# A decoder layer on one core: early tiles and late gates in the front, split score exponentials and shared row work at the end

## The chip, the cores and the metric

The kernel runs on one core of a Trainium2 chip. TensorE (PE) does the matmuls and transposes, VectorE (DVE) and ScalarE (ACT) the element-wise work and the evacuation of PSUM, GpSimd (POOL) part of the element-wise work in SBUF, and SyncE (SP) issues most of the DMAs. The metric is the device time of one execution in microseconds (us), as the median of several runs.

## The reference

One decoder layer in fp32, for 16 sequences `x` of 512 × 256, with a context of 64 × 128 for each. `_layernorm` is a layernorm without weights.

```python
# 1. long-convolution block with a gated MLP (FF = 672)
z = rmsnorm(u, pre_norm_w) @ in_proj_w.T              # 256 -> 768 channels
z_pre = depthwise_causal_conv3(z, short_w) + short_b
x2, x1, v = split(z_pre, 3)
h = sum(residues[:, :, None] * exp(log_poles * t), axis=1)   # 16 poles a channel
xv = x1 * v
y = (causal_conv(xv, h) + xv * D_skip) * x2           # x2 is the gate
y = y @ out_proj_w.T + u
zm = rmsnorm(y, post_norm_w)
y = y + gelu(zm @ l1_w.T) * (zm @ l2_w.T) @ l3_w.T
x = _layernorm(x + y)
# 2. causal self attention plus cross attention (16 heads of 16)
y = softmax(causal(q k^T) / 4) v + softmax(qc kc^T / 4) vc
x = _layernorm(x + y @ Wp + bp)
# 3. low-rank FFN: 256 -> 64 -> 1024 -> 64 -> 256
x = _layernorm(x + gelu(x @ U1 @ V1 + b1) @ U2 @ V2 + b2)
```

## The kernel before

**Two plans.** The order of the work is not written by hand. Each step is an operation with the engines that may run it, an estimated cost, a priority (a lower number goes first), and the buffers that it reads and writes. `Plan.schedule` simulates the engines with these costs, and each engine's instructions are emitted in the order found; each engine then runs its queue in order, with semaphores between engines. A buffer comes from a class with a fixed number of tiles, and an operation starts only when a tile of its class is free. So a change of priority, of engine or of the number of tiles moves other work too.

**The front plan** does all that goes before sequence 0 can run. `prepare` (L440) loads x, normalises it and transposes it to `xT`. `project` (L473) makes one of six slices of 128 channels: two matmuls of 512 (L479, two records each, so four records for one projection), an ACT evacuation (L486), and two DVE steps of the short convolution (L494). `x1v` (L502) takes two projections, multiplies them on POOL (L506), transposes the product on PE (L512) and copies it into `xv`, kept on chip. `gate_of` (L523) takes two projections of x2 and stores them to DRAM (`gates`). Poles and residues give the table `h` (L607 to L637: 32 exponentials on ACT, L613, and 32 multiply-adds on DVE, L623), which is stored to DRAM as `hpad`.

The long convolution (L648 to L774) runs in eight blocks, four for each half kh of the channels. A block loads four Toeplitz tiles ("toes", 512 KB each) from `hpad` (L661), clears their upper part on POOL (L671), and runs the near states (L686, then L696, L706 and L714), the exponentials of the far part (L722), the toe matmuls (L737) and the far matmuls (L749); the result is copied to a row and stored to DRAM (`yconv`, L768). Half kh = 0 runs among the projections. Half kh = 1 needs the `xv` of all sequences.

The class `"x"` has ten tiles of 4 KB a partition (`fx` in the profile). It holds the loaded x, the `xT`, and the toes. The last nine sequences (LATE) have only their first x1·v made early, and the last five (KEPT) keep their `xT` until the second one. The gates of sequences 14 and 15 (LAST) are made after the convolution. In the last part of kh = 1 the toes also use the first half of `xv`, which is finished then (class `"x0"`).

**The main plan** pipelines the sequences: `first_block` (loads of x, gate and the two halves of `yt`, gating at L1105, output projection L1118, MLP L1143 to L1195), `attention` and `ffn`, each in a later window, so that three sequences are under way. In attention, `scores` is one tile of four PSUM banks (128 × 2048). A round is: PE writes the scores (L1491; L1552 in the cross attention), ACT takes the exponential of the whole tile into one of three `ex` tiles (L1503, L1563), POOL clears the part above the diagonal (L1514), and PE multiplies by the values (L1526, L1578). The next round's scores need the same tile. A sequence has twelve rounds (ten of L1491, two of L1552). `to_tokens` (L1056) projects the result back, and `layernorm_ops` (L1019) ends each block: statistics on DVE, the inverse root on POOL (L308, L309), the scaling of four rows of tokens on ACT (L1041). `ffn` (L1689) has transposes (L348), L1704, four pairs of blocks (two L1716 into two `mm` banks, two gelus at L1724 on ACT, two L1732 into `av`), and L1745. The last sequence has no later one beside it.

Of the kernel before, what the change touches and what calls it, by code (L numbers as in the profile page):

```python
# [10 lines left out]
AF = mybir.ActivationFunctionType  # L11
# [186 lines left out]
def decoder_layer(  # L198
# [77 lines left out]
    def tiles(home, name, n, shape):  # L276
        return [home.tile(shape, F32, name=f"{name}{k}") for k in range(n)]
# [88 lines left out]
    R8 = 8  # L366
    NR = D // HPG
    with ExitStack() as front:
        fp_ = front.enter_context(tc.tile_pool(name="front", bufs=1))
# [4 lines left out]
            "mm": tiles(fps, "fmm", 8, [P, T]),  # L374
            "x": tiles(fp_, "fx", 10, [P, R8 * P]),
            "far": tiles(fp_, "far", 1, [P, R8, P]),
# [59 lines left out]

        def as_xT():
            return View("x", lambda t: t.rearrange("p (k n) -> p k n", k=KD))

        def prepare(b, pr):  # L440

            x_ = View("x", lambda t: t.rearrange("p (c d) -> p c d", c=NT))
            for c in range(0, NT, 1 if b == 0 else NT):
                cs = slice(c, c + (1 if b == 0 else NT))
                plan.op(
                    "SP", 0.5 if b == 0 else 0.5 * MB,
                    lambda e, cs=cs: nc.sync.dma_start(
                        out=x_.t[:, cs, :], in_=x[b].rearrange("(c p) d -> p c d", p=P)[:, cs, :]
                    ),
                    pr - 1000, w=[(x_, c)] if b == 0 else [x_], lat=2.5, after=at_step(b - 3),  # L450
                )
            if b == 0:
                load_in(prew, pre_w, -900, [(INW, "p")])
                for k in range(KD):
                    load_in(inw[:, k, :], in_wT[bass.ts(k, P), :], -900, [(INW, k)])
                load_in(cw, conv_w, -890, [(CW, 0)])
                load_in(cb, conv_b, -890, [(CW, 1)])
                for k in range(KD):
                    plan.op(
                        "DVE", 0.9,  # L460
                        lambda e, k=k: nc.vector.tensor_scalar(
                            inw[:, k, :], inw[:, k, :], prew[:, k : k + 1], None, ALU.mult
                        ),
                        -900, r=[(INW, "p")], w=[(INW, k)],
                    )

            sq = rms_ops(x_, pr - 120)
            scale_ops(x_, sq, pr - 120, "POOL" if b else "DVE")
            xT = transposed(x_, lambda t: t, pr - 120, as_xT())
            marks.append(plan.ops[-1])  # L470
            return xT
# [85 lines left out]
        for b, xT in late:  # L557
            if b < B - KEPT:
                xT = as_xT()
                plan.op(  # L560
                    "SP", 0.5 * MB,
                    lambda e, b=b, xT=xT: nc.sync.dma_start(
                        out=xT.t.rearrange("p k n -> p (k n)"), in_=normed[b - B + LATE]
                    ),
                    1900 + b, r=[(NORMED, b)], w=[xT], lat=2.5, after=at_step(B - 1 - 2 * (b % 2)),
                )
            late_T.append((b, xT))
            x1v(b, 1, xT, 3000 + b * 100)
            marks.append(plan.ops[-1])
            if b < B - LAST:  # L570
                gate_of(b, xT, 3000 + b * 100)
        last_gates = []
# [34 lines left out]
        for k in range(KD):  # L607
            h = Buf("h")
            for n in range(NS):
# [5 lines left out]
                    ),  # L615
                    160, r=[(LP, 0)], w=[ee],
                )
# [10 lines left out]

                plan.op("DVE", 0.32, add, 160, r=[ee, (LP, 1), (LP, 2)], w=[h])
            plan.op(  # L630
                "SP", 0.4, lambda e, k=k, h=h: nc.sync.dma_start(out=hpad[bass.ts(k, P), :], in_=h.t), 160,
                r=[h], w=[(HPAD, k)], lat=3.0,
            )
        plan.op(
            "SP", 0.4, lambda e: nc.sync.dma_start(out=hpad[D : D + 1, :], in_=zero_row), 160, w=[(HPAD, KD)],
            lat=3.0,
# [9 lines left out]
        plan.op("ACT", 0.4, lambda e: nc.scalar.activation(aT, lpT, AF.Exp, scale=float(P)), 170, r=[(LP, "T0")], w=[(NEAR, "a")])  # L646

        for blk in range(NR // R8):  # L648
            d0 = blk * R8 * HPG
# [105 lines left out]
            for c in range(HPG):  # L755
                o = View("row", lambda t: t.rearrange("p (q u) -> p q u", u=P))
                plan.op(
                    "ACT DVE", (act(T), dve(T)),
                    lambda e, c=c, o=o, ys=ys: copy(
                        e, o.t, ys[c].t.rearrange("p (q u) -> p q u", u=P)[:, :, ::-1]  # L760
                    ),
                    pc + 5, r=[ys[c]], w=[o],
                )
                for par in range(2):

                    def store(e, at=x0 + c * R8 + par * R8 // 2, par=par, kh=kh, o=o):
                        eng = nc.sync if e == "SP" else nc.scalar
                        eng.dma_start(  # L768
                            out=yconv[kh].rearrange("j b d t -> (j b) d t")[:, at : at + R8 // 2, :],
                            in_=o.t[bass.ts(par, 64)],  # L770
                        )


                    plan.op("ACT" if par and blk >= NR // R8 - 3 else "SP", 0.6, store, pc + 10, r=[o], lat=3.0)  # L774

# [204 lines left out]
        "maxes": tiles(kept, "maxes", 2, [P, NT, HPG, SLOT]),  # L980
        "yt": tiles(kept, "yt", 1, [P, KD, T]),
        "gate": tiles(kept, "gate", 1, [P, KD * T]),
        "y1": tiles(kept, "y1", 1, [P, NT, D]),
        "xt": tiles(kept, "xt", 5, [P, NT, D]),
        "xT": tiles(kept, "xT", 3, [P, KD, T]),
# [32 lines left out]

    def layernorm_ops(x, prio, at_once=NT):  # L1019
        for c0 in range(0, NT, at_once):  # L1020
# [16 lines left out]
            for c in range(c0, c0 + at_once):  # L1037

                def norm(e, c=c, small=small):
                    st = small.t  # L1040
                    nc.scalar.activation(  # L1041
                        x.t[:, c, :], x.t[:, c, :], AF.Identity, bias=st[:, c, 9:10], scale=st[:, c, 8:9]
                    )

                plan.op("ACT", act(D, True) + 0.05, norm, prio, r=[small], w=[(x, c)])

# [33 lines left out]
    def first_block(b, after):  # L1080
# [15 lines left out]

        plan.op("SP", 0.5, load_x, p0 - 500, w=[x_], lat=4.0)
        plan.op("SP", 0.5, load_g, p0 - 500, w=[gate], lat=4.0)
        for k in range(KD):
            plan.op("SP", 0.5, lambda e, k=k: load_y(e, k), p0 - 500, w=[(yt, k)], lat=4.0)  # L1100
# [106 lines left out]
    def attention(b, x_):  # L1207
# [241 lines left out]
        def shifted(g):  # L1449
# [8 lines left out]
            for gg in range(g, g + 2):  # L1458
                q = qs[gg]
                qas[gg], cqas[gg] = Buf("q"), Buf("q")  # L1460
                for row, dst in ((self_rows[gg % 2], qas[gg]), (cross_rows[gg % 2], cqas[gg])):
# [6 lines left out]
                    )  # L1468

        def sums(g0):  # L1470

# [10 lines left out]
            for uses in fills:  # L1482
# [3 lines left out]
                def mm(e, uses=uses, sc=sc):  # L1486
                    at = 0
                    for g, j in uses:
# [11 lines left out]
                ))  # L1500
                exps[b + 1].append(plan.op(
                    "ACT", act(HPG * T),
                    lambda e, sc=sc, ex=ex: nc.scalar.activation(  # L1503
                        ex.t.rearrange("p (r n) -> p r n", r=HPG), sc.t, AF.Exp, scale=scale
                    ),
                    pb_ - 5, r=[sc], w=[ex],
                ))
                at = 0
# [34 lines left out]
        def cross_scores(g):  # L1543
# [4 lines left out]
            def cm(e):  # L1548
                for r in range(HPG):
# [10 lines left out]
            ))  # L1560
            exps[b + 1].append(plan.op(
                "ACT", act(HPG * T),
                lambda e: nc.scalar.activation(  # L1563
                    ex.t.rearrange("p (r n) -> p r n", r=HPG), sc.t, AF.Exp, scale=scale
                ),
                pb_ - 5, r=[sc], w=[ex],
            ))

# [116 lines left out]
        to_tokens(yT, wp_s, x_, p3)  # L1685
        layernorm_ops(x_, p3, NT // 2 if b == B - 1 else NT)
        return begun

    def ffn(b, x_):  # L1689
# [18 lines left out]

        acc = Buf("av")
        for fp in range(NH // 2):  # L1710
            hp = [Buf("mm"), Buf("mm")]

            def hm(e, fp=fp, hp=hp):
                for s in range(2):
                    half = bass.ts(s, RANK)
                    nc.tensor.matmul(hp[s].t, v1_s[half, bass.ts(fp, P)], pT.t[half, :], start=True, stop=True)  # L1716

            gelus_pe[window].append(plan.op("PE", tiled(T), hm, p3, r=[pT], w=hp, tiling=ROWS2))
            hT = [Buf("row"), Buf("row")]
            for s in range(2):  # L1720
                f = 2 * fp + s
                gelus[window].append(plan.op(
                    "ACT", act(T, True),
                    lambda e, f=f, src=hp[s], dst=hT[s]: nc.scalar.activation(  # L1724
                        dst.t, src.t, AF.Gelu_apprx_tanh, bias=b1_s[:, f : f + 1]
                    ),
                    p3, r=[hp[s]], w=[hT[s]],
                ))
# [23 lines left out]
        n = NT // halves  # L1752
        layernorm_ops(x_, p4, n)
        for c0 in range(0, NT, n):
# [112 lines left out]
```

## Time and profile before

| | |
|---|---|
| median of the runs | 2112.74 us (2112.03, 2112.74, 2116.0) |
| profiled execution, its own time | 2110.95 us |
| its span in the profile | 2109.2 us |
| mean TensorE clock granted in the profiled execution | 0.987 of full |
| PE busy | 2013.7 us, 95% of the span |
| DVE busy | 1317.1 us, 62% |
| ACT busy | 1020.7 us, 48% |
| POOL busy | 758.2 us, 36% |
| DMA | 182.16 MB, 86 GB/s on average |
| second half of the convolution, first L686 | at 247.78 us |
| first L1118 (sequence 0) | at 292.07 us |
| first and last start of the last sequence's score rounds | 2019.51 and 2060.12 us |

The profile is of one execution. The slices give each engine's busy share in tenths in 40 equal parts of the span, 52.7 us each; PEclk is the granted clock of TensorE. A row of the timeline gives start, duration, engine, source line, operation, output and inputs, shapes and the number of instructions put together (xN); in square brackets stands the idle time ahead of it and what ended it. The chain of waits runs back from the last instruction to what released each step. The busy table by stage has one row for each stretch, and the busy time of each engine in it.

### The profile page before, as it was taken

How to read it: one execution, taken by the hardware profiler on the slowest of the kernel's cores; microseconds unless marked ns; L12 is line 12 of the kernel's file. 1: busy time of each engine (PE TensorE's matmuls, PEld its weight loads, DVE VectorE, ACT ScalarE, POOL GpSimd, SP SyncE). 2: the span in 40 equal slices, each digit the busy share in tenths (PEclk: the TensorE clock that was granted, in tenths of full speed). 3: DMA queues.
4: the chain of work that ended last, by engine and by line, in shares of the span. 5: the costliest groups of instructions: out<-in, count | busy, mean ns of one | idle time of the engine just before them, and what ended most of it. 6: DMA issues, size and time to landing. Idle time of an engine off the chain costs nothing.

```text
span 2109.2 us, 35600 instructions
## 1 busy us (share of the span) xinstructions
PE 2013.7 (95%) x14324; PEld 1034.7 (49%) x14324; DVE 1317.1 (62%) x1899; ACT 1020.7 (48%) x1414; POOL 758.2 (36%) x1020
## 2 busy tenths in 40 slices
PE   8899878999999999999999999999999999999977
PEld 4455545444554545454545454544545454545433
DVE  7976522736584848484847575766656675746463
ACT  7764521565426262717172626262535354466664
POOL 6785522243424241414141424242323232334342
PEclk9999989999999999999999999999999999999999
DMA  5366861030304040313131313222221313030300
GB/s 190 112 199 210 272 191 50 1 122 17 117 11 140 14 132 22 122 32 120 34 109 45 106 48 93 61 86 68 72 81 61 93 49 95 19 105 22 102 11 21
DMA packets 114935, 182.16 MB, mean 86 GB/s; under 512 B 13393, under 2 KB 62034, under 8 KB 114642
## 3 DMA queue, kind: packets, MB, share of 16 engines
q1 hardware_dynamic: 113234, 177.26, 27.0%
q10 hardware_dynamic: 1536, 2.62, 0.4%
q8 instruction: 113, 1.85, 0.4%
q14 instruction: 52, 0.43, 0.1%
HBM read 111.09 MB, written 68.76 MB: 85 GB/s over the span
## 4 chain that ended last, share of the span: by engine, by line
PE 81%; ACT 7%; POOL 4%; DVE 3%; issue 3%; DMA 2%; SPq 0%; ACTq 0%; POOLq 0%; DVEq 0%
PE mm L1143 14%; PE scores L1387 10%; PE mm L1296 9%; PE mm L1195 8%; PE scores L1491 7%; PE av L1526 7%; PE mm L1716 4%; PE mm L1224 3%; PE av L1732 3%; PE mm L1056 3%; PE fmm L479 2%; ACT ex L1503 2%; PE mm L1118 2%; PE mm L348 2%; PE mm L1578 2%
## 5 line engine op out<-in xcount | busy, mean ns | idle before, releaser
L1503 ACT ACTIVATE ex<-scores 128x2048 f32<-128x2048 f32 x160 | 300.2, 1876 | 165.4 <-PE scores L1491 161.3
L1143 PE MATMUL mm<-xT,w_l 128*128 128x512 f32 x640 | 298.1, 607 | 0.0
L1514 POOL TENSOR_SCALAR_AFFINE_SELECT ex<-ex 128x512 f32<-128x512 f32 x256 | 158.6, 638 | 355.2 <-ACT ex L1503 330.8
L1387 PE MATMUL scores<-keys,q 32*128 32x320 f32 (+4 forms) x2560 | 224.2, 455 | 11.8 <-ACT ex L1406 10.4
L1491 PE MATMUL scores<-q,keys 32*128 32x512 f32 (+3 forms) x2048 | 185.0, 464 | 17.3 <-ACT ex L1503 14.2
L1724 ACT ACTIVATE row<-mm,b_s 128x512 f32<-128x512 f32 x128 | 81.0, 685 | 233.0 <-PE mm L1716 232.9
L1143 PEld LDWEIGHTS mm<-xT,w_l 128*128 128x128 f32 x640 | 114.9, 190 | 143.7 <-issue 130.8
L1387 PEld LDWEIGHTS scores<-keys,q 32*128 32x128 f32 x2560 | 113.0, 184 | 147.2 <-issue 48.0
L1660 POOL TENSOR_TENSOR nd<-nd,nd 128x1024 f32<-128x1024 f32 x30 | 70.8, 2361 | 307.4 <-DMA nd<-di 307.4
L479 PE MATMUL fmm<-fx,inw 128*128 128x512 f32 x384 | 176.5, 602 | 4.1 <-DVE xv L299 1.5
L1526 PE MATMUL av<-ex,va 128*32 128x512 f32 (+3 forms) x2048 | 170.8, 442 | 0.0
L1432 DVE TENSOR_TENSOR scores<-scores,mask_qk 128x1024 f32<-128x1024 f32 x144 | 126.2, 876 | 63.8 <-PE scores L1387 60.6
L308 POOL TENSOR_SCALAR small<-small 128x4 f32<-128x4 f32 (+1 forms) x66 | 13.3, 201 | 423.0 <-DVE small L1026 393.7
L494 DVE SCALAR_TENSOR_TENSOR frow<-fmm,cw,frow 128x511 f32<-128x511 f32 x192 | 140.5, 744 | 37.7 <-ACT frow L486 33.5
L1195 PE MATMUL mm<-w_l,gT 128*128 128x256 f32 x640 | 160.8, 386 | 0.0
L1155 ACT ACTIVATE row<-mm 128x512 f32<-128x512 f32 x80 | 47.8, 598 | 223.9 <-PE mm L1143 223.9
L1491 PEld LDWEIGHTS scores<-q,keys 32*128 32x128 f32 x2048 | 90.0, 185 | 117.4 <-ACT ex L1503 42.2
L299 DVE COPY row<-av 128x512 f32<-128x512 f32 x68 | 47.1, 692 | 157.9 <-PE av L1526 136.2
L1195 PEld LDWEIGHTS mm<-w_l,gT 128*128 128x128 f32 x640 | 117.8, 190 | 47.3 <-issue 33.7
L1041 ACT ACTIVATE xt<-xt,small 128x256 f32<-128x256 f32 x192 | 103.1, 595 | 76.6 <-POOL small L1034 76.6
L1302 DVE TENSOR_SCALAR q<-mm,bqc_s 128x512 f32<-128x512 f32 x62 | 46.5, 751 | 140.6 <-PE mm L1296 140.6
L1296 PE MATMUL mm<-xT,wqc_s 128*128 128x512 f32 x256 | 129.3, 617 | 0.0
(194 smaller groups left out, 3475.4 us busy)
## 6 DMA issues: line engine op xcount, KB each, us to landing
dn<-row SPq DMA_DIRECT2D x120, 256.0 KB
keys<-dk SPq DMA_DIRECT2D x64, 256.0 KB
nd<-dn SPq DMA_DIRECT2D x30, 512.0 KB
nd<-di SPq DMA_DIRECT2D x30, 512.0 KB
fx<-hpad SPq DMA_DIRECT2D x28, 512.0 KB
xt<-in_x SPq DMA_DIRECT2D x16, 512.0 KB
gate<-gates SPq DMA_DIRECT2D x16, 512.0 KB
yt<-yconv SPq DMA_DIRECT2D x32, 256.0 KB
```

The lines of the kernel that those rows point to most:

```text
L479: nc.tensor.matmul(ps.t, inw[:, k, bass.ts(m, P)], xT.t[:, k, :], start=(k == 0), stop=(k == KD - 1))
L494: lambda e, lag=lag: nc.vector.scalar_tensor_tensor(t.t[:, lag:], ps.t[:, 0 : T - lag], cw[:, m, 2 - lag : 3 - lag], t.t[:, lag:], ALU.mul ...
L1041: nc.scalar.activation(x.t[:, c, :], x.t[:, c, :], AF.Identity, bias=st[:, c, 9:10], scale=st[:, c, 8:9])
L1143: nc.tensor.matmul(ps.t, w[:, k, bass.ts(f, P)], zT.t[:, k, :], start=(k == 0), stop=(k == KD - 1))
L1195: nc.tensor.matmul(ps.t[:, bass.ts(cc, D)], gT.t[:, f, bass.ts(c, P)] if f < NF else gE.t, w_l3[:, f, :] if f < NF else w_l3e[:, c, :], st ...
L1296: nc.tensor.matmul(ps.t, w[:, k, cols], xT.t[:, k, :], start=(k == 0), stop=(k == KD - 1))
L1387: nc.tensor.matmul(sc.t[:, r, at : at + hi - lo], q.t[hd, bass.ts(i, P)], kk.t[hd, lo:hi], start=True, stop=True,)
L1432: nc.vector.tensor_tensor(diag, diag, mask, ALU.add)
L1491: nc.tensor.matmul(sc.t[:, r, at : at + T - j * P], keys[g].t[hd, TC + j * P : TC + (j + 1) * P], qas[g].t[hd, j * P :], start=True, stop= ...
L1503: lambda e, sc=sc, ex=ex: nc.scalar.activation(ex.t.rearrange("p (r n) -> p r n", r=HPG), sc.t, AF.Exp, scale=scale),
L1514: lambda e, ex=ex, at=at: nc.gpsimd.affine_select(out=ex.t.rearrange("p (r n) -> p r n", r=HPG)[:, :, at : at + P], in_=ex.t.rearrange("p ...
L1526: nc.tensor.matmul(av[g].t[bass.ts(r, SLOT), j * P :], va.t[:, j, h * VS : h * VS + SLOT], ex.t[:, r * T + at : r * T + at + n], start=(j ...
```

## The change

1. Three tiles of 4 KB a partition, `early`, are allocated outside the front's pool. In the front plan they hold the `xT` of sequences 11, 12 and 13. In the main plan they are one of the five `xt` tiles, the `gate` tile and the `yt` tile. The class `"x"` has 7 tiles instead of 10.
2. The exponentials, multiply-adds and stores of the `h` table have priority 500 instead of 160.
3. The gates of sequences 10 to 13 have priority 4700 + 100 b instead of 3000 + 100 b, and the second half of the convolution has 5000 and up.
4. Sequence 0's x, gate and the first half of its `yt` are loaded by DMAs in the front plan, after the last readers of the early tiles and after the stores that they need; the main plan's operations for them are empty, and it loads the second half of `yt`.
5. In the last sequence, each exponential of a scores tile is split: ACT takes the first two banks from PSUM; DVE copies the other two to the `ex` tile, and ACT takes their exponential there.
6. In the last sequence, the scaling of rows after attention and after the FFN may run on ACT or DVE. For sequence 14's FFN it runs on DVE.
7. In the last FFN, the first two pairs of L1716 write to the four banks of the scores tile.

```diff
+    early_ = ctx.enter_context(tc.tile_pool(name="early", bufs=1))
+    early = tiles(early_, "early", 3, [P, NT * D])
...
-            "x": tiles(fp_, "fx", 10, [P, R8 * P]),
+            "x": tiles(fp_, "fx", 7, [P, R8 * P]),
+            **{f"e{n}": [t] for n, t in enumerate(early)},
...
-        def as_xT():
-            return View("x", lambda t: t.rearrange("p (k n) -> p k n", k=KD))
+        def as_xT(b):
+            n = b - (B - KEPT)
+            return View(f"e{n}" if 0 <= n < 3 else "x", lambda t: t.rearrange("p (k n) -> p k n", k=KD))
...
-                gate_of(b, xT, 3000 + b * 100)
+                gate_of(b, xT, (3000 if b < B - LAST - 4 else 4700) + b * 100)
...
-                    160, r=[(LP, 0)], w=[ee],
+                    500, r=[(LP, 0)], w=[ee],
...
+        for n, (dst, src, deps) in enumerate((
+            (early[0].rearrange("p (c d) -> p c d", c=NT), x[0].rearrange("(c p) d -> p c d", p=P), ()),
+            (early[1], gates[0], (stores[0][1], stores[1][1])),
+            (early[2].rearrange("p (k j t) -> p k j t", k=KD, j=NT)[:, 0],
+             yconv[0][:, 0].rearrange("j p t -> p j t"), Y[0]),
+        )):
+            plan.op(
+                "SP", 0.6, lambda e, dst=dst, src=src: nc.sync.dma_start(out=dst, in_=src), 5460, w=[Buf(f"e{n}")],
+                lat=4.0, after=[*deps, *(o for _, o, _ in late_T[LATE - KEPT + n][1].seen)],
+            )
...
-        "yt": tiles(kept, "yt", 1, [P, KD, T]),
-        "gate": tiles(kept, "gate", 1, [P, KD * T]),
+        "yt": [early[2].rearrange("p (k n) -> p k n", k=KD)],
+        "gate": [early[1]],
...
-        "xt": tiles(kept, "xt", 5, [P, NT, D]),
+        "xt": [early[0].rearrange("p (c d) -> p c d", c=NT), *tiles(kept, "xt", 4, [P, NT, D])],
...
+                    if e == "DVE":
+                        nc.vector.tensor_scalar(
+                            x.t[:, c, :], x.t[:, c, :], st[:, c, 8:9], st[:, c, 9:10], ALU.mult, ALU.add
+                        )
+                        return
...
-                plan.op("ACT", act(D, True) + 0.05, norm, prio, r=[small], w=[(x, c)])
+                cost = {"ACT": act(D, True) + 0.05, "DVE": dve(D)}
+                plan.op(on, tuple(cost[e] for e in on.split()), norm, prio, r=[small], w=[(x, c)])
...
-        for k in range(KD):
+        plan.op("SP", 0.5, load_x if b else lambda e: None, p0 - 500, w=[x_], lat=4.0)
+        plan.op("SP", 0.5, load_g if b else lambda e: None, p0 - 500, w=[gate], lat=4.0)
+        if not b:
+            plan.op("SP", 0.5, lambda e: None, p0 - 500, w=[(yt, 0)], lat=4.0)
+        for k in range(0 if b else 1, KD):
...
+        def exponentials(sc, ex, prio):
+            direct, half = (HPG, None) if b < B - 1 else (HPG // 2, HPG // 2)
+            def exp(e, src, rs):
+                dst = ex.t.rearrange("p (r n) -> p r n", r=HPG)
+                nc.scalar.activation(dst[:, rs, :], (sc.t if src else dst)[:, rs, :], AF.Exp, scale=scale)
+            if half:
+                rest = slice(direct, HPG)
+                plan.op(
+                    "DVE", dve(half * T),
+                    lambda e: nc.vector.tensor_copy(
+                        ex.t.rearrange("p (r n) -> p r n", r=HPG)[:, rest, :], sc.t[:, rest, :]
+                    ),
+                    prio, r=[(sc, 1)], w=[(ex, "half")],
+                )
+            exps[b + 1].append(plan.op(
+                "ACT", act(direct * T), lambda e: exp(e, True, slice(0, direct)), prio, r=[(sc, 0)] if half else [sc],
+                w=[(ex, "first")] if half else [ex],
+            ))
+            if half:
+                exps[b + 1].append(plan.op("ACT", act(half * T), lambda e: exp(e, False, rest), prio, w=[ex]))
...
-        layernorm_ops(x_, p3, NT // 2 if b == B - 1 else NT)
+        layernorm_ops(x_, p3, *((NT // 2, "ACT DVE") if b == B - 1 else ()))
...
-        acc = Buf("av")
+        acc, sc4 = Buf("av"), Buf("scores")
...
-            hp = [Buf("mm"), Buf("mm")]
+            in_scores = last and fp < 2
+            hp = [(sc4, 2 * fp + s) for s in range(2)] if in_scores else [Buf("mm"), Buf("mm")]
...
-        layernorm_ops(x_, p4, n)
+        layernorm_ops(x_, p4, n, "ACT DVE" if last else "DVE" if window > B else "ACT")
```

## The prediction, made before the changed kernel ran

> **What bounds it now.** First the page's slices (part 2): which engine is full, and where it is not.
>
> ```profile
> PE   8899878999999999999999999999999999999977
> ...
> PEclk9999989999999999999999999999999999999999
> DMA  5366861030304040313131313222221313030300
> ```
>
> TensorE (PE) is full but for slices 0 to 6 (to 316 us) and the last two, so a gain must come out of the two ends, and only what PE waits for counts there. The middle keeps its order on every engine in the built program. Second, the busy table by stage (columns: us, busy time of PE, PEld, DVE, ACT, POOL, then clock, DMA share, GB/s).
>
> ```profile
> 230.00:236.00 6.00, 6.00 (x18) 2.86 (x17) 5.40 (x8) 5.46 (x13) 1.27 (x1) 1.00 0.89 229
> 236.00:241.00 5.00, 4.56 (x11) 1.71 (x9) 4.62 (x7) 4.41 (x12) 2.85 (x3) 1.00 1.00 386
> 241.00:248.00 7.00, 1.99 (x21) 1.38 (x24) 3.65 (x5) 1.83 (x6) 6.55 (x7) 0.69 0.99 395
> 248.00:255.00 7.00, 6.77 (x201) 6.41 (x195) 1.11 (x2) 0.00 (x0) 5.30 (x10) 0.82 0.66 247
> ...
> 284.00:292.00 8.00, 0.00 (x0) 0.00 (x0) 3.89 (x6) 0.29 (x1) 0.00 (x0) 0.75 0.96 328
> 292.00:300.00 8.00, 6.75 (x16) 5.10 (x16) 2.08 (x3) 1.37 (x6) 0.00 (x0) 0.61 0.99 330
> ```
>
> There are two holes: 241 to 248, ahead of the second convolution half, and 284 to 292, ahead of sequence 0. DMA is nearly full in both. Third, PE's timeline names the waits.
>
> ```profile
> 241.62 0.66 PE L512 MATMUL fmm<-ident,frow 128*128 128x128 f32 x4 [1.07 <-POOL frow L506]
> 245.44 1.12 PE L512 MATMUL fmm<-ident,frow 128*128 128x128 f32 x4 [3.16 <-POOL frow L506]
> 247.78 2.79 PE L686 MATMUL fmm<-xv,near 128*32 128x48 f32 x128 [1.22 <-DVE xv L299]
> ...
> 275.90 7.13 PE L479 MATMUL fmm<-fx,inw 128*128 128x512 f32 x16
> 292.07 6.75 PE L1118 MATMUL mm<-outw,yt 128*128 128x256 f32 x16 [9.04 <-DVE yt L1105]
> ```
>
> Fourth, the chain of waits: the first hole hangs on a Toeplitz load (then POOL's L671 and L506), the second on the read of yconv.
>
> ```profile
> 236.12 6.80 DMA fx<-hpad
> ...
> 283.62 7.53 DMA yt<-yconv
> ```
>
> Last, PE and ACT at the other end, where the last sequence has only part of a partner's work beside it.
>
> ```profile
> 2053.70 1.14 PE L1491 MATMUL scores<-q,keys 32*128 32x512 f32 x8 [1.06 <-ACT ex L1503]
> 2056.90 1.15 PE L1491 MATMUL scores<-q,keys 32*128 32x384 f32 x16
> ```
> ```profile
> 2054.97 1.88 ACT L1503 ACTIVATE ex<-scores 128x2048 f32<-128x2048 f32 x1 [1.32 <-POOL ex L1514]
> 2058.20 1.88 ACT L1503 ACTIVATE ex<-scores 128x2048 f32<-128x2048 f32 x1 [1.35 <-PE scores L1491]
> 2080.02 2.06 ACT L1041 ACTIVATE xt<-xt,small 128x256 f32<-128x256 f32 x4
> 2083.64 1.07 ACT L301 COPY xT<-mm 128x512 f32<-128x512 f32 x2 [1.56 <-PE mm L348]
> ```
>
> With one scores tile, a round is scores 1.15, exp 1.88 and two hand-overs: 3.2 us, as the starts 2053.70 and 2056.90 show. Eight of the twelve rounds stand at this floor; the others wait for other work.
>
> **Front.** The sum is made against the profiled execution: 2110.95 us, span 2109.2 and 1.75 around it; it lies 1.79 below the median of 2112.74. A projection is four L479 records: 7.13 / 4 = 1.78 us.
>
> *Late gates.* In the built order four projections fewer stand ahead of the second half's first L686 (247.78): −7.1 us. Two gates (10, 11) now stand between the last x1·v steps, where PE idled 1.07 + 3.16 + 1.22 = 5.45: up to −12.5 for that start. Two things can take it back: POOL's queue, since L506 stands behind L671, which waits for toes (4.36 us behind the load above), and the DMA queues. In 230 to 248 DMA work is 6×0.89 + 5×1.00 + 7×0.99 = 17.3 of 18 us; four gate stores of 256 KB (1.0 MB at 390 GB/s, 2.7 us) and about three prefetched toes of 512 KB (4.0 us) leave it, so 10.6 us is left for the 5.5 us that PE's work would need there. The other 5.1 has to go ahead of 230, where shares of 0.86 (180 to 205) and 0.79 (205 to 230) leave 8.75 us free. It fits with little to spare, so I take −11, from −12.5 to −4.
>
> *Convolution.* One projection (gate 12) now stands inside the half: +1.8. The cold start goes: the clock was 0.69, then 0.82; 0.18 of 7 us is about −1. With x at 7 tiles instead of 10, five x buffers and x0 feed the half instead of eight and x0. The built order gives a buffer some 8 us of PE work between uses; a load takes 6.30 or 6.80 us in the chain, and L671 1.09, so I take +1.2 for those that come late, 0 to +6. Sum +2.
>
> *After it.* Before, convolution's end to L1118 is 292.07 − 275.90 = 16.2 us, 7.1 of it four projections. Now seven follow, 12.5 us. The first loads of sequence 0 (x, gate, half of yt) have gone out earlier; only yt's second half is left, on SP behind two gate stores (ready some 8 us in), and it should land about 11.7 us in; L1105 (0.70) follows. I take 13.5: −2.7 (−4 to 0). The moved gate load waits on SP for gate 12's last L479, 1.8 us after the convolution's PE end; behind it are yconv stores, thus row buffers, the evacuations and PE. Bound 0 to +2, taken inside the 13.5. With no hole in front, the 16 L1118 cost 4.81, as in the later group at 346.85, not 6.75: −1.9.
>
> *Early part.* PE idles about 9 us from 30 to 175, of which 5.4 lies in 55 to 71, where the h tables (L613, 32 × 395 ns; L623, 30 × 414 ns) fill ACT and DVE. Given later priority they can release that; three tiles fewer can delay the input loads by one landing, about 4. Bounds −5 and +4; I take 0, as both act on the same queue.
>
> Front: −11 + 2 − 2.7 − 1.9 = −13.6.
>
> **End.** *Split exponentials.* No row shows a 1024-wide exp; between 587 ns (512 wide) and 1876 ns (2048) the line gives 1.02 us. The nearest row for the DVE copy of two banks is L1432's 128x1024 on the scores tile, 1.23. In the built order the halves do not run side by side: in each round one waits on the other's semaphore, and PE's next scores on both. The banks are held 1.02 + 1.23 + 0.06 = 2.31 instead of 1.88: +0.43, in eight floor rounds +3.5 (0 if other work sets them, +6 with all twelve and one half exp more at the end).
>
> *Shared rows.* The second norm batch (small ready 2080.48) can start the transposes at 2081.1 instead of 2083.01: −1.9 (0 to −2.3). Of the two xT copies in a row (1.07) one goes to DVE: −0.4. *FFN blocks in score banks:* the last FFN runs 2087.5 to 2097.2. Four pairs of gelus at 1.27 are 5.1 of it, norms of sequence 14 between them 2.3, which leave ACT; but the first gelu waits for four L1716 rather than two, +1.1: −1.2 (−2.3 to +1). Final norms 1.09 to 0.60: −0.5. Sum −4.0.
>
> End: +3.5 − 4.0 = −0.5; ends −4 (split free) and +5 (split dear, little shared).
>
> Two rules of the skill weigh on the end. The row: in 2019.5 to 2024.9 the clock was 0.50 and eight score records took 2.09 us, with single waits of PE of 1.99 and 3.32 us around them; in 2050.5 to 2053.7, PE busy 2.14 of 3.20, it was 1.00 and they took 1.15. The Trainium skill, "TensorE: Matmul & The Clock Gate", section "Part 1: The HAM clock gate", halves the clock only after a whole idle window of about 3.4 us; by it, longer rounds stay warm and cost nothing more. By the row a sparse stretch can be cold: 12 × 0.94 = +11 at worst. The new round, 2.14 of 3.63, is nearer to the warm row (67% busy) than to the cold one (39%), so I add none; one cold round, +0.9, is inside the end's +5. "PSUM — Partial Sum Buffer", section "PSUM bank collisions raise a hardware error", lets two engines work on different banks at once; by that rule, halves side by side would hold the banks 1.23 and bring 8 × −0.65 = −5.2. No run here shows it, and the built waits speak against it.
>
> **The sum.** −13.6 − 0.5 = −14.1: 2110.95 − 14.1 = 2096.9 on the profiled execution's basis, 2112.74 − 14.1 = 2098.6 on the median's, which I give. About 0.2% (4.2 us) can be told from no change.
>
> **Rivals.** *Both ends gain* (0.14): the split costs nothing because AV, row scalings and POOL's masks set the rounds, and the early part gives 4: −13.6 − 4 − 4 = −21.6, 2091.1. For it: four rounds already stand off the floor. Against: eight do not.
>
> *DMA is the bound of the front* (0.14): share 0.99 at 395 GB/s in the hole means the hole is a transfer's, and the gates fill it without moving its end. Then the start moves by 4, the convolution loses 3, and yt's read (7.53 us at share 0.96) takes back 1 of the 2.7: −4 + 3 − 1.7 − 1.9 = −4.6; with the end's −0.5 that is −5.1, 2107.6. Half of this lies within 0.2%.
>
> *The toes starve* (0.10), slower: one mechanism, the time between two uses of an x buffer. Each of six generations of buffers (four in the first half, two in the second) loses what landing and L671 exceed the 8 us by. At 6.8 nothing much is lost; at 9.2 us it is 2.3 × 6 = 14 and the gain is gone: the deciding point; at 10.2 the loss is 20: 2112.74 − 14.1 + 20 = 2118.6. For it: POOL waits 3.62 and 4.36 us for fx now, with three tiles more. Against: buffers of finished x tiles return in the second half.
>
> Forecast 0.62, its own range 2092 to 2105. Range over the cases: 2090 to 2112; outside it lie the slower rival and the tail of the faster one. Faster 0.62 + 0.14 + 0.07 = 0.83, same 0.07, slower 0.10.
>
> **What would show it.** First L1118 at about 278 instead of 292.07, after a wait of about 1 us and lasting 4.8; the second half's first L686 (the wide one) at 237, with no wait over 1 us ahead; clock 1.00 there; fx landings still 6 to 7 us. At the end, score starts 3.6 apart, each half exp after the copy or ahead of it, never beside it. It is wrong if L1118 starts after 287, if the fx landings exceed 9, or if the rounds stay at 3.2 or pass 4.2.

## The result, and the profile after

The changed kernel ran in 2106.64 us (median of 8 runs, 2102.59 to 2110.3) against 2112.47 for the kernel before (8 runs, 2111.25 to 2117.05): a ratio of 0.9971, 95% interval 0.9962 to 0.998, so 5.8 us faster, less than half of the 14.1 that was forecast. The profiled execution took 2108.62 us (span 2106.9, clock 0.986), 2.0 above its own median.

First the page's slices of the changed kernel.

```profile
PE   8999978899999999999999999999999999999977
```

Both ends are still thin. The PE timeline of the changed kernel around the second half of the convolution (L485 is the old L479, L694 the old L686, L745 the toe matmuls, L757 the far ones, L1148 the old L1118):

```profile
234.98 1.57 PE L694 MATMUL fmm<-xv,near 128*32 128x48 f32 x128
...
241.39 3.65 PE L745 MATMUL fmm<-fx,xv 128*64 128x128 f32 x37 [2.30 <-issue]
...
266.70 5.42 PE L485 MATMUL fmm<-early,inw 128*128 128x512 f32 x12
271.95 7.03 PE L485 MATMUL fmm<-fx,inw 128*128 128x512 f32 x16
283.34 2.04 PE L1148 MATMUL mm<-outw,early 128*128 128x256 f32 x4 [4.36 <-DVE early L1135]
286.43 4.51 PE L1148 MATMUL mm<-outw,early 128*128 128x256 f32 x12 [1.05 <-DVE early L1135]
```

The first hole is gone: the half begins at 234.98 instead of 247.78, without a wait ahead of it and warm (1.57 us instead of 2.79; warm and cold are short for matmuls at the full granted clock and at a lower one). The second hole is not: between the last projection and L1148 PE still waits 4.36 and 1.05 us where it had waited 9.04, and L1148 is cold again, 2.04 + 4.51 = 6.55 us. The chain of waits of the changed kernel says what it hangs on:

```profile
259.31 5.29 DMA early<-in_x
...
266.18 3.93 DMA gates<-frow
...
271.34 4.93 DMA yconv<-frow
276.33 4.33 DMA yconv<-frow
280.75 4.84 DMA early<-yconv
```

It runs through SP's queue from one transfer to the next: the early load of x, then gate stores and yconv stores, and only then the read of yt. VectorE's timeline shows the other side of that queue, a copy that waits for a row until an old store has landed:

```profile
265.78 0.69 DVE L299 COPY frow<-fmm 128x512 f32<-128x512 f32 x1 [3.77 <-DMA yconv<-frow]
```

At the other end, DVE, ACT, PE and the busy table by stage of the changed kernel:

```profile
2051.26 1.22 DVE L1512 COPY ex<-scores 128x1024 f32<-128x1024 f32 x1 [1.37 <-ACT ex L1506]
```
```profile
2052.52 1.02 ACT L1506 ACTIVATE ex<-scores 128x1024 f32<-128x1024 f32 x1 [1.38 <-DVE ex L1512]
...
2053.90 1.07 ACT L1506 ACTIVATE ex<-ex 128x1024 f32<-128x1024 f32 x1
```
```profile
2049.95 1.14 PE L1545 MATMUL scores<-q,keys 32*128 32x512 f32 x8
...
2053.59 1.15 PE L1545 MATMUL scores<-q,keys 32*128 32x384 f32 x16 [0.70 <-ACT ex L1506]
...
2063.84 2.31 PE L1620 MATMUL mm<-ex,vc 64*32 64x512 f32 x16 [1.95 <-ACT row L1771]
2066.08 1.97 PE L1779 MATMUL av<-row,u_s 128*64 128x512 f32 x4
```
```profile
2060.00:2064.00 4.00, 1.23 (x17) 0.68 (x10) 1.37 (x3) 3.97 (x5) 0.00 (x0) 1.00 0.02 4
2064.00:2068.00 4.00, 4.00 (x21) 0.49 (x19) 0.69 (x1) 0.95 (x2) 0.00 (x0) 0.59 0.00 0
```

A round is 3.64 us (2049.95 to 2053.59) instead of 3.20: ACT's half waits for DVE's copy (which ends at 2052.48; ACT begins at 2052.52), and PE for ACT's half. And the first matmuls behind the rounds are cold: L1620 2.31 and L1779 1.97 us at a clock of 0.59, where they had been 1.09 and 1.08.

### The profile page after: what moved, and what is told of

It reads as the page before. It is cut to its first block, busy times and chain, and to the rows that moved or that the text cites. A ratio compares the mean times of both kernels' runs of the same rounds, so it can differ in the third digit from the quotient of the medians.

```text
span 2106.9 us, 35589 instructions
## 1 busy us (share of the span) xinstructions
PE 2017.9 (96%) x14324; PEld 1034.4 (49%) x14324; DVE 1340.5 (64%) x1924; ACT 1015.4 (48%) x1413; POOL 757.2 (36%) x1020
## 4 chain that ended last, share of the span: by engine, by line
PE 84%; ACT 7%; POOL 3%; DVE 2%; DMA 2%; issue 2%; SPq 0%; POOLq 0%; DVEq 0%; ACTq 0%
PE mm L1173 14%; PE scores L1417 10%; PE mm L1326 9%; PE mm L1225 8%; PE scores L1545 7%; PE av L1574 7%; PE fmm L485 5%; PE mm L1763 3%; PE av L1779 3%; PE mm L1254 3%; PE mm L1083 3%; ACT ex L1506 2%; PE mm L1148 2%; PE mm L348 2%; PE mm L1620 2%
## 5 line engine op out<-in xcount | busy, mean ns | idle before, releaser
L1506 ACT ACTIVATE ex<-scores 128x2048 f32<-128x2048 f32 (+1 forms) x192 | 350.1, 1823 | 193.5 <-PE scores L1545 152.5
L1771 ACT ACTIVATE row<-mm,b_s 128x512 f32<-128x512 f32 x124 | 78.5, 686 | 233.5 <-PE mm L1763 233.4
L485 PE MATMUL fmm<-fx,inw 128*128 128x512 f32 x312 | 143.5, 604 | 0.0
L1436 ACT COPY ex<-scores 128x2048 f32<-128x2048 f32 x48 | 89.6, 1866 | 56.5 <-PE scores L1417 49.6
```

Of the source, the lines that this page charges most:

```text
L485: nc.tensor.matmul(ps.t, inw[:, k, bass.ts(m, P)], xT.t[:, k, :], start=(k == 0), stop=(k == KD - 1))
L1436: "ACT", act(HPG * T), lambda e, sc=sc, both=both: nc.scalar.copy(both.t, sc.t), ps_ - 6,
L1506: nc.scalar.activation(dst[:, rs, :], (sc.t if src else dst)[:, rs, :], AF.Exp, scale=scale)
```

## The experiments

The table holds, for every kernel, the median and its ratio to the kernel before in the same runs (95% interval), and from one profiled execution each: the start of the second half's first near states (L694), the end of its last far matmul, the first L348 of sequence 0 (from there on the middle is the same in all, 1715.4 to 1717.5 us to the last sequence's first scores), the time from those scores to the start of the last L1620, and from there to the end of the span. All in us.

| kernel | median | ratio | L694 | conv. end | L348 | rounds | behind |
|---|---|---|---|---|---|---|---|
| before | 2112.5 | | 247.8 | 276.0 | 304.0 | 45.8 | 43.9 |
| changed | 2106.6 | 0.9971 (0.9962 to 0.998) | 235.0 | 266.8 | 296.1 | 50.6 | 43.1 |
| e1 | 2101.2 | 0.9945 (0.9932 to 0.9958) | 236.3 | 267.4 | 295.1 | 46.3 | 40.9 |
| e2 | 2102.0 | 0.9946 (0.9933 to 0.9959) | 230.0 | 261.9 | 287.0 | 50.5 | 44.1 |
| e3 | 2106.5 | 0.9974 (0.9964 to 0.9985) | 235.9 | 272.1 | 298.6 | 51.4 | 42.9 |
| e4 | 2108.4 | 0.9986 (0.9975 to 0.9996) | 239.1 | 273.8 | 302.5 | 50.5 | 44.2 |
| e5 | 2093.4 | 0.9922 (0.9908 to 0.9935) | 232.9 | 264.2 | 288.1 | 45.7 | 41.0 |
| e6 | 2104.1 | 0.9967 (0.9954 to 0.9979) | 233.9 | 269.2 | 293.8 | 46.7 | 43.9 |
| e7 | 2097.1 | 0.9934 (0.9921 to 0.9946) | 233.0 | 266.7 | 295.1 | 43.0 | 40.6 |
| e8 | 2115.8 | 1.002 (1.0011 to 1.0029) | 246.0 | 274.7 | 299.7 | 51.8 | 42.7 |
| e9 | 2093.0 | 0.9906 (0.9891 to 0.9922) | 235.5 | 265.6 | 294.5 | 42.0 | 42.3 |
| e10 | 2110.9 | 0.9993 (0.9985 to 1.0002) | 233.5 | 266.7 | 296.5 | 50.5 | 44.1 |
| e11 | 2103.9 | 0.9957 (0.9944 to 0.9971) | 233.7 | 265.0 | 291.0 | 52.4 | 42.9 |

The runs were made in four sets, and the median of the kernel before differs among them: 2112.5 beside the changed kernel, 2112.2 beside e1 to e4, 2111.2 beside e5 to e8, 2112.1 beside e9 to e11. So a difference of two medians from different sets can be off by 1.3 us; the ratios leave that out.

The changed kernel, e1, e6 and e7 have the same order on PE and SP in the front, and their L694 starts lie between 233.0 and 236.3, their L348 between 293.8 and 296.1; e2, with PE's order unchanged, began its L694 at 230.0, before anything that it changes. Among the same four the convolution takes 31.1 to 35.4 us and the way from its end to L348 24.6 to 29.3; their sum, from L694 to L348, is steadier, 58.8 to 62.1 (56.2 before). Nor is the profiled execution always near the median: it lies 5.3 and 6.5 above it in e3 and e4, 3.2 above in e9, and 2.2 to 2.6 below in e2, e6, e8 and e10. So one execution says little about a difference under 4 us in the front, and the verdicts there rest on medians. The rounds at the end vary less: 45.7 to 46.7 in the four kernels with whole exponentials, 50.5 to 52.4 in the seven that split one tile, 43.0 and 42.0 in the two with two tiles.

**e1: whole exponentials in the last sequence.**

```diff
-            direct, half = (HPG, None) if b < B - 1 else (HPG // 2, HPG // 2)
+            direct, half = HPG, None
```

> The changed kernel with whole exponentials in the last sequence too (part 5 undone; all else as changed; the front's order is the same on PE). Theory A, the serial halves set the rounds: from the first score round of the last sequence to its last L1620 the span goes from 50.6 us back to about 45.8, and the cold matmuls behind it (L1620 2.31, L1779 1.97) to about 1.1 each, so the end is shorter by 4.5 to 6.5 us and the kernel about 2101. Rival: the rounds are longer because VectorE's shared rows stand ahead of the score work; then the span stays within 1.5 us of 50.6 and the kernel within 2 us of the changed one.

2101.2, 5.4 below the changed kernel. PE's timeline of e1:

```profile
2046.74 1.14 PE L1545 MATMUL scores<-q,keys 32*128 32x512 f32 x8 [1.05 <-ACT ex L1506]
2049.94 1.15 PE L1545 MATMUL scores<-q,keys 32*128 32x384 f32 x16
...
2058.38 1.09 PE L1620 MATMUL mm<-ex,vc 64*32 64x512 f32 x16 [1.45 <-ACT row L1771]
```

The round is 3.20 again, the rounds together are 4.2 us shorter, and L1620 is warm. The split is what makes the end slower, by its rounds and by the cold matmuls behind them: the last L1620 takes 1.09 us in all four kernels with whole exponentials and 2.31 to 2.54 in all seven that split one tile.

**e2: yt read first.** The second half of yt is read by the front's own plan, as soon as its stores are done; x of sequence 0 and the gate stores of 12 and 13 go behind it.

```diff
+            if not n:
+                continue
...
+        yt1 = plan.op(
+            "SP", 0.6,
+            lambda e: nc.sync.dma_start(
+                out=early[2].rearrange("p (k j t) -> p k j t", k=KD, j=NT)[:, 1],
+                in_=yconv[1][:, 0].rearrange("j p t -> p j t"),
+            ), 5460, w=[dst_], lat=4.0, after=Y[1],
+        )
+        x_first = plan.op(
+            "SP", 0.6,
+            lambda e: nc.sync.dma_start(
+                out=early[0].rearrange("p (c d) -> p c d", c=NT), in_=x[0].rearrange("(c p) d -> p c d", p=P)
+            ), 5460, w=[Buf("e0")], lat=4.0, after=[yt1, *(o for _, o, _ in late_T[LATE - KEPT][1].seen)],
+        )
+        for b_, o_ in stores:
+            if b_ in (12, 13):
+                o_.deps.add(x_first)
...
```

> The changed kernel with another order of SP's transfers at the end of the front, PE's order there unchanged: both halves of yt are read as soon as their stores are done, then x of sequence 0, then the gate stores of sequences 12 and 13. The bytes are the same. Theory A, the transfers ahead of the yconv stores on SP delay yt (about 1.5 MB, 4.6 us at the 329 GB/s of 275 to 292): the last L1148 group begins 3 to 5 us earlier than 286.4, the kernel is at 2102 to 2104. Rival, the convolution and the evacuations set when the stores can go, not the queue: under 1 us.

2102.0, 4.7 below the changed kernel, with intervals that do not overlap. The bytes are the same in all, but fewer stand ahead of L1148: from the end of the convolution to its first group the DMA engines moved 250 GB/s at a share of 0.80 for 13.4 us, in the changed kernel 301 GB/s at 0.95 for 16.6 us. PE's timeline of e2 (L1167 is L1148):

```profile
275.35 1.38 PE L1167 MATMUL mm<-outw,early 128*128 128x256 f32 x4 [1.22 <-DVE early L1154]
277.41 2.86 PE L1167 MATMUL mm<-outw,early 128*128 128x256 f32 x12 [0.69 <-DVE early L1154]
```

The last group begins 15.5 us after the end of the convolution instead of 19.7, and is warm: 1.38 + 2.86 = 4.24 us. That alone would not show the cause, since the execution has a part in it: in e6, with the changed kernel's order, the last group begins after 16.5 us and is warm too, and in e9, with the order of e2, it begins after 18.0 us and is cold (0.67 + 5.80). The medians carry the verdict: e5 against e1 (7.8 us) and e9 against e7 (4.1 us) repeat the gain with the other ends, and by the ratios the three gains are 5.3, 4.9 and 5.9 us.

**e3: gate stores on ScalarE's queue.**

```diff
-                    "SP", 0.25 * MB,
-                    lambda e, m=m, t=t: nc.sync.dma_start(out=gates[b][:, bass.ts(m, T)], in_=t.t), pr,
+                    "SP" if pr < 4000 else "ACT", 0.25 * MB if pr < 4000 else 0.6,
+                    lambda e, m=m, t=t: (nc.sync if e == "SP" else nc.scalar).dma_start(
+                        out=gates[b][:, bass.ts(m, T)], in_=t.t), pr,
```

> The changed kernel with the gate stores of sequences 10 to 13 issued on ScalarE's queue instead of SP's; same bytes, nearly the same moments. Theory A1, SP's issue (0.5 to 1.1 us for each transfer, each waiting for an earlier one's landing) is the limit: L1148's last group begins 3 us or more earlier. Theory A2, the transfers themselves are (DMA share 0.99 from 275 to 292): within 1 us of 286.4.

2106.5, no difference: the 3 us of theory A1 are not there. The profile does not say why. It is of an execution 5.3 us above the median, and PE's order is not quite the same: one more gate projection stands inside the convolution, which takes 36.2 us instead of 31.8, and one fewer behind it (26.5 to L348 instead of 29.3). So this does not separate issue from transfer.

**e4: first loads back in the main plan.** The front's loads are removed, and the main plan's are real again.

```diff
-        for n, (dst, src, deps) in enumerate((
+        for n, (dst, src, deps) in enumerate(() and (
...
-        plan.op("SP", 0.5, load_g if b else lambda e: None, p0 - 500, w=[gate], lat=4.0)
+        plan.op("SP", 0.5, load_g, p0 - 500, w=[gate], lat=4.0)
...
-        for k in range(0 if b else 1, KD):
+        for k in range(KD):
```

> The changed kernel with part 4 undone: gate and both halves of yt of sequence 0 are loaded by the main plan, after the front's stores, as before; x goes out early. PE's front order is the same. If the early loads are worth what I took (16.2 us after the convolution becoming 13.5 with seven projections instead of four), undoing them costs 2 to 4 us at L1148. Theory A: the early loads only move bytes ahead of the yconv stores, and undoing them costs under 1 us or gains up to 2.

2108.4, 1.8 slower than the changed kernel, with intervals that overlap. So the early loads, as the change placed them, gained about 2 us by the medians (3 by the ratios), and not even that is clear of the noise.

**e5: the edits of e1 and e2 together.**

> Whole exponentials (as in e1) and the transfer order of e2 together. If the two costs are separate, one at each end, they add: 2106.6 - 5.4 - 4.7 = about 2096.5, with the last L1148 group about 15.6 us after the end of the convolution, score rounds of 46 us and 41 us behind them. Rival: part of what e2 showed is chance of the front's loads (its convolution also began 5 us earlier with the same orders); then the sum stays above 2099.

2093.4, 3 below what the two gains add up to by medians; by the ratios they add up to 0.9920, against 0.9922 measured. The costs at the two ends are separate ones.

**e6: the front alone.** The edit of e1, and parts 6 and 7 undone.

```diff
-        layernorm_ops(x_, p3, *((NT // 2, "ACT DVE") if b == B - 1 else ()))
+        layernorm_ops(x_, p3, NT // 2 if b == B - 1 else NT)
...
-            in_scores = last and fp < 2
+            in_scores = False
...
-        layernorm_ops(x_, p4, n, "ACT DVE" if last else "DVE" if window > B else "ACT")
+        layernorm_ops(x_, p4, n)
```

> Parts 1 to 4 of the change alone, with the end as it was before (whole exponentials, row scalings on ScalarE, the last FFN in the mm banks). Theory: the front gave 6 to 8 us, not 13.6, so 2104 to 2106; score rounds 45.8, 43.9 behind them as before. Against e1 (2101.2) it prices parts 6 and 7, from the profiles 2.9 us. Rival: the end's new order costs elsewhere too, then it is below 2102.

2104.1 against 2111.2 in the same runs: the front gave 7.1. Against e1, parts 6 and 7 give 2.8 by medians, with intervals that overlap, and the profiles agree: 43.9 us behind the rounds against 40.9. PE's timeline of e6 shows how the front differs from one execution to the next:

```profile
269.17 7.22 PE L485 MATMUL fmm<-early,inw 128*128 128x512 f32 x12
...
283.09 1.03 PE L1148 MATMUL mm<-outw,early 128*128 128x256 f32 x4
285.71 2.86 PE L1148 MATMUL mm<-outw,early 128*128 128x256 f32 x12 [1.59 <-DVE early L1135]
```

The order on PE is the changed kernel's, but the cold stretch stands elsewhere: the end of the convolution and the projections behind it are slow (the twelve L485 take 7.22 us instead of 5.42), and L1148 is warm.

**e7: two tiles for the halves.** The scores tile of four banks is released after its last use, and two tiles of two banks take its place in the last sequence.

```diff
+    def last_scores():
+        if not pairs:
+            sc_home.close()
+            p2 = ctx.enter_context(tc.tile_pool(name="sc2", bufs=1, space=PSUM, reuse_waits="tile"))
+            pairs.extend(tiles(p2, "pair", 2, [P, HPG // 2, T]))
+        return pairs
...
-                nc.scalar.activation(dst[:, rs, :], (sc.t if src else dst)[:, rs, :], AF.Exp, scale=scale)
+                from_ = last_scores()[0] if src and b == B - 1 else (sc.t if src else dst)[:, rs, :]
+                nc.scalar.activation(dst[:, rs, :], from_, AF.Exp, scale=scale)
...
```

> The changed kernel with the halves of the last sequence's scores in two PSUM tiles of two banks instead of one of four (the same banks; the pair takes the place of the old tile after its last use). In the built order a half then waits for its own scores alone, not for the other half's reader. Theory: the split is dear only because the halves are serial. Side by side a round is 1.15 + 1.23 + hand-overs, about 2.6 us, unless POOL or AV are later: rounds 43 to 46 us instead of 50.6, kernel 2099 to 2102. Rival: two engines reading PSUM and the queues of VectorE and POOL keep the rounds over 49.

2097.1, 9.5 below the changed kernel (7.8 by the ratios). Against e1 it is 4.1 below by medians and 2.3 by the ratios, with intervals that overlap. The timelines of ACT, DVE and PE in e7:

```profile
2045.01 1.02 ACT L1518 ACTIVATE ex<-pair 128x1024 f32<-128x1024 f32 x1 [0.77 <-PE pair L1557]
```
```profile
2045.08 1.23 DVE L1524 COPY ex<-pair 128x1024 f32<-128x1024 f32 x1 [1.33 <-PE pair L1557]
```
```profile
2043.77 1.14 PE L1557 MATMUL pair<-q,keys 32*128 32x512 f32 x8
...
2046.63 1.15 PE L1557 MATMUL pair<-q,keys 32*128 32x384 f32 x16
```

The two engines read the same round's scores at once (2045.01 and 2045.08), each in the time that it takes alone, and this round is 2.86 us instead of 3.64. The same split costs time with one tile (rounds of 50.5 us and more, against 45.7 to 46.7 with whole exponentials) and shortens the rounds with two (43.0).

**e8: the gates where they were.**

```diff
-                gate_of(b, xT, (3000 if b < B - LAST - 4 else 4700) + b * 100)
+                gate_of(b, xT, 3000 + b * 100)
```

> The changed kernel with part 3 undone: the gates of sequences 10 to 13 have their old priority and come before the second half of the convolution. If late gates carry the front's gain, the convolution's second half begins 7 to 11 us later than 235 and the first L348 3 to 6 us later than 296: 2110 to 2112. Rival, DMA is the bound of the front wherever the gates stand: what is lost ahead of the convolution comes back behind it, and the time is within 1.5 us of 2106.6.

2115.8, slower than the changed kernel and than the kernel before. PE's timeline of e8 has the first hole back:

```profile
241.09 0.66 PE L518 MATMUL fmm<-ident,frow 128*128 128x128 f32 x4 [3.34 <-POOL frow L512]
...
245.98 2.79 PE L694 MATMUL fmm<-xv,near 128*32 128x48 f32 x128 [1.21 <-DVE xv L299]
```

So late gates carry the front's gain. And with the same seven x tiles the convolution takes 274.7 − 246.0 = 28.7 us, against 28.2 with ten, which is no difference that one execution can show.

**e9: the edits of e7 and e2 together.**

> The two-tile halves of e7 and the transfer order of e2 together. If they are separate, 2097.1 - 4.7 to - 7.8 (what the order was worth in e2, and in e5 against e1) = 2089 to 2092.5, below e5's 2093.4. Rival: the two-tile end shares nothing with the front but may lose its lead to a cold clock behind the rounds (L1620 1.66 in e7): 2093 or more.

2093.0, the fastest beside e5. Its lead over e5 is 0.4 by medians and 3.4 by the ratios, with intervals that overlap, so the medians do not show that two tiles are better than whole exponentials. That the two gains add is likely: the ratios of e7 and e2 together make 0.9909, and e9 has 0.9906. In its profile, 3.2 us above its median, the rounds are the shortest of all (42.0), but L348 comes at 294.5 and L1620 takes 1.99.

**e10: the h table early again**, on all four lines of part 2.

```diff
-                plan.op("DVE", 0.32, add, 500, r=[ee, (LP, 1), (LP, 2)], w=[h])
+                plan.op("DVE", 0.32, add, 160, r=[ee, (LP, 1), (LP, 2)], w=[h])
...
```

> The changed kernel with part 2 undone: the h table's exponentials, multiply-adds and stores at priority 160 again. Theory: the 3 us by which the first half's near states begin earlier (172.5 against 175.5) come from moving the table's work, so they go: near states at 175 to 176, kernel 2108.5 to 2110. Rival: the 3 us come from elsewhere (the early tiles' places), then 172 to 173 and within 1 us of 2106.6.

2110.9, 4.2 slower than the changed kernel; the first half's near states begin at 175.7, as before, instead of 172.5. The busy table, first of the changed kernel, then of e10, shows where PE loses them:

```profile
60.00:90.00 30.00, 30.00 (x100) 15.22 (x98) 29.14 (x47) 25.69 (x61) 23.06 (x26) 1.00 0.23 77
```
```profile
60.00:90.00 30.00, 26.65 (x88) 13.06 (x87) 27.34 (x42) 23.36 (x56) 26.16 (x30) 1.00 0.33 110
```

PE is busy for 3.35 us less in this stretch. But the profiled execution, 2.2 below its median, has made it up by the second half, which begins at 233.5, no later than the changed kernel's. So the medians show that the late table is worth about 4 us, and the profile does not show where they come out.

**e11: e2 with the early load of x left where the change put it.** The edit is shown against e2.

```diff
-            if not n:
-                continue
...
-                o_.deps.add(x_first)
+                o_.deps.add(yt1)
```

> As e2 (yt read as soon as it is stored, gate stores of sequences 12 and 13 behind it), but the load of x of sequence 0 stays where the change put it, ahead of 16 of the second half's yconv stores. If the early x load is what delays the stores (in the changed kernel's chain of waits, early<-in_x 5.29 us, then the stores), the gain over the changed kernel is 2 us or less; if the gate stores are, it is 4 us or more, as in e2.

2103.9, 2.8 below the changed kernel where e2 was 4.7 below, between the two expectations. Its interval overlaps both that of e2 and that of the changed kernel, so how much of e2's gain belongs to the gate stores and how much to the place of x stays open.

## Why the prediction was half right

**Late gates and the start of the half: right.** Taken −11, measured −12.8 at L694. e8 shows that it is the gates: undoing them alone moves the start back by 11.0 us, with an uncertainty of some 3 us between executions.

**Early part: taken 0, measured −3.0** at the first half's near states. The two bounds were there (−5 and +4), but they did not cancel: e10 shows that the h table's later place gives the 3 us there, and 4.2 in the medians; with the table early and seven tiles the near states begin at 175.7 against 175.5, so the fewer tiles cost nothing like a landing.

**Convolution: taken +2, measured +3.6** (31.8 against 28.2) in this execution, and +2.9 to +7.2 in the four with the same order. The gate in the half takes 1.9 of it; the rest, waits and a lower clock, was not parted. Seven tiles without that gate (e8) took 28.7. The fear that the toes come late, the slower rival, is refuted: the three fx loads in the changed kernel's chain of waits land in 4.6 to 6.8 us.

**After it: taken −2.7 and −1.9, measured +1.3. This step failed**, and it is the largest miss in the profile: 5.9 of the 8.3. I set yt's landing at 11.7 us after the convolution by PE's work and two gate stores, and counted the moved loads as taken off the path. I did not price what else stands ahead of it on SP. The last yt read was issued at 280.75, 14.0 us after the convolution's end, and landed 4.84 later. In the chain the moved load of x (5.29), gate stores and yconv stores stand ahead of it, and rows are not free until the stores have landed (3.77 us on DVE). e2 puts the same bytes into another order and gets 4.7 us back, of the 6.5 by which the front fell short (13.6 taken, 7.1 in e6). I had named the wait of the gate load and what is queued behind it; what counted stood ahead of yt on the same queue, the gate stores that the change itself had made late and the load of x. e11 does not part these two.

Where the loss shows is one execution's: in e6 the convolution has it (+7.2) and the way behind it is 3.4 shorter than before, with the clock down earlier there (0.83 of full from 250 to 269 us, against 1.00 in the changed kernel from 250 to 267). What holds in all is the sum from L694 to L348. I took +2 − 2.7 − 1.9 = −2.6 for it; the four kernels with this order have +2.6 to +5.9, and e2, e5 and e9, with the other order, −0.9 to +2.9. The −1.9 for a warm L1148 has the same fate: it is cold in the changed kernel and warm in e6.

**The split: sign and size of a round right, the sum wrong.** The floor round grew by 0.44, forecast 0.43. The rounds together grew by 4.7 and not by 3.5, but not because more of them paid. I had counted eight at the floor; six of the eleven spacings are at 3.15 to 3.23 us, and two more at 3.53 and 3.58. These six grew by 4.0 together, the other five became 0.6 shorter, and the last round's way to L1620 grew by 1.4, which I had only in the upper bound. The matmuls behind them went cold, 2.31 + 1.97 against 1.09 + 1.08, another 2.1 us, which I had at nothing. Together 6.8 in the profile and 5.4 in the medians (e1), taken +3.5.

**The clock.** I added nothing for it, and the row beside it spoke for the cold case: half speed in a stretch whose longest wait was 3.32 us. Here PE waited 0.81 and 1.95 us, was busy 1.23 of the 4.00 us from 2060 to 2064, and ran at 0.59 in the next 4. The Trainium skill's "TensorE: Matmul & The Clock Gate", section "Part 1: The HAM clock gate", with one whole idle window of about 3.4 us ahead of the slow clock, would not have it cold; the measurement decides.

**Two engines on one scores tile.** The Trainium skill's "PSUM — Partial Sum Buffer", section "PSUM bank collisions raise a hardware error", lets two engines use different banks at once. e7 agrees with it: 1.02 and 1.23 us side by side. So what kept them apart in the changed kernel was the waits built for one tile of four banks, and not the banks, which are the same in e7.

**Shared rows and FFN blocks: taken −4.0, measured −2.9** in the profiles (e6 against e1) and −2.8 in the medians. From the first L1716 of the last FFN to its last L1745 it was 10.43 us and is 9.91, so the score banks gave 0.5 instead of 1.2. The first gelu waits 2.0 us from the first L1716 on instead of 1.2, near the +1.1 that I had taken for four blocks; where the other 0.7 went was not tried.

By medians, front −7.1 (e6), parts 6 and 7 −2.8 (e1 against e6), split +5.4 (the changed kernel against e1): −4.5, against a measured −5.8. The 1.3 between them is the difference between the sets of runs; as the three are links of one chain, their sum is no test of them. The rival with the DMA as the bound of the front came out at 2107.6, next to the result, but by another way: it let the start move by 4 only. The start moved in full, and the transfers took much of it back behind the start, through their order on the queue; that the number came near is luck.

## What to carry to other kernels

When work is moved out of a hole, look at the next hole on the same path and list every transfer of the queue that ends it, in the order of issue: a load that is "already out" can stand ahead of the one that is waited for. Sharing a tile between two engines is only sharing if the waits are built per engine's part; give each half a tile of its own. A term that is "per round" has an end, too: what the last round does later, and what runs cold behind it, belong to it. And where neighbouring stages share a queue, price them together and by medians, since one execution can have the loss in either.

## What the runs showed of the hardware

ScalarE and VectorE read different banks of PSUM at the same time without slowing each other (1.02 and 1.23 us for 128x1024, together as alone). TensorE's clock fell to 0.59 behind a stretch with waits of 0.81 and 1.95 us only, and the matmul group there took 2.31 to 2.54 us instead of 1.09 in all seven kernels with that stretch. And another order of the same transfers on one queue was worth 4.7 us (e2).
